# A fused Flamingo block on one core: first alignment part of 12 sequences instead of 16, the second part's dense work as a hand-ordered pipeline with its clamp on GpSimd

## The chip, the core and the metric

The kernel runs on one core of a Trainium2 chip. The core has five engines with in-order queues of their own: TensorE (PE; its weight loads are listed as PEld), VectorE (DVE), ScalarE (ACT), GpSimd (POOL) and SyncE (SP, here only a queue for DMAs). DMAs are issued from SP, ACT and POOL. The metric is device microseconds of one launch; lower is better.

## The reference, cut to what matters

Input are 32 sequences of 128 tokens with 128 features. Four residual steps follow each other, each on the row-normalised state.

```python
x = x + tanh(g_xattn[0]) * mlstm_attention(_layernorm(x), ctx)      # step 1
x = x + tanh(g_ffn[0])   * quantised_ffn(_layernorm(x), W1, b1, W2, b2)   # step 2
x = x + tanh(g_xattn[1]) * align(ctx, _layernorm(x))                # step 3
x = x + tanh(g_ffn[1])   * moe(_layernorm(x), gate_w, w1, b1, w2, b2)     # step 4
```

- Step 2 quantises its input and its hidden values with one scale for the whole tensor: `q = clip(round(h / scale) + zp, -128, 127)`, and multiplies the integers.
- Step 3 is dynamic time warping for every sequence: a 128x128 matrix of distances `sqrt(max(aa + bb - 2 ab, 0))`, the recursion `R[i,j] = d[i,j] + min(R[i-1,j], R[i,j-1], R[i-1,j-1])`, and a backtrack along the cheapest path, which adds context rows to tokens.
- Step 4 is a mixture of 8 experts (128 to 512 to 128 with gelu). Every expert is computed for every token. The gate keeps logits from a k-th value upwards, and that k-th value is taken over all tokens, so gates are known only when step 3 is done for all 32 sequences.

## The kernel before, in words

Sequences are handled in groups of four (`GB`), eight groups (`NG`). Features or hidden units lie on the 128 partitions; `X` holds the state, `YT` the transposed normalised state, `CT` and `CD` the context.

Up to 228 us steps 1 and the first half of step 2 are done for all 32 sequences. Then the sequences are split: the first `NP` groups (4 before, 16 sequences) are the first part, the rest the second.

1. **First dense part** (`dense_steps`, with `dense`, `norm_steps`, `take` and `distances`). For each group of the first part: quantise 128x2048 hidden values (`HT`) on DVE (L905), ACT (L908) and DVE (L909), multiply on PE (L915), add to `X` on DVE (L920), normalise (L153 to L209), transpose, make distances on PE (L930, L932) and their roots on ACT (L938 to L941), and write these to DRAM (`d_dram`, L944).
2. **First warp** (`warp_steps`). Every sequence is worked from both ends, so the recursion has 64 rows (`SH`), and both halves of n sequences lie on 2n partitions. Rows come in `CHUNKS`. Each row is two DVE instructions that depend on each other: a minimum (L1035) and a scan (L1036). The distances of a chunk are loaded by DMA (`dc`, L1019). After a chunk, its rows (`ru`) are spread by four DMAs over 128 partitions (`rblk`, L1045), DVE works out step lengths in a few wide instructions (`dg`, `to`, `lf`, `vv`, `dv`, L1061 to L1074; called a block here) and DMAs bring them back (L1076). `rblk` is a single buffer. After the last row `meet` joins the two halves (PE L978 and L984, copies `gt` and `far` on ACT, L981 and L990, ten small DVE instructions). Then 63 DVE instructions walk back (`hit`, L1084), and `ends` is worked out through PE (L1092 to L1106).
3. **Second dense part** (`quiet`), issued beside the first warp. It leaves DVE alone: ACT does the whole quantisation in four passes of 128x2048 (L1151, L1153, L1155, L1156), PE multiplies (L1160), ACT scales (`t`, L1165), GpSimd adds to `X` (L1167), ACT takes mean and square sums (L1173, L1177), GpSimd the root (L1181 to L1183), ACT normalises (L1187), PE transposes (L1190), and `distances` follows. One group starts when the one before has finished its roots.
4. **Mixture of experts.** `aligned(g)` applies the path to group g and gives its logits. Then PE runs 64 units (expert times group), 8 experts for the first part's groups and 8 for the second's. Second warp, alignments of the other groups and the search for the k-th value are fed in between as a background (`pump`), with a budget in microseconds per step given by `yield`. Results of the first `HELD` units go to DRAM until the gates are known.

What sets the order: every engine executes its queue strictly in the order in which a planner, which orders instructions by estimated times, has put them; `tc.issue_after(...)` ties an instruction behind another. An instruction that waits holds back everything behind it on its queue, also where it is a DMA on ACT's or SP's queue.

Of the kernel before, what the change touches and what calls it, by code (L numbers as in the profile page):

```python
# [18 lines left out]
P = 128  # L19
B = 32  # L20
# [13 lines left out]
SH = S // 2  # L34
CHUNKS = ((0, 16), (16, 16), (32, 16), (48, 8), (56, 8))
NP = 4
BP = NP * GB
HELD = 32


@with_exitstack
def tile_flamingo_gated(
# [747 lines left out]
    parts = [ExitStack(), ExitStack()]  # L790
    HT = [None, None]
    for k in (1, 0):
        HT[k] = new(
            pool(parts[k], f"ffn{k}", side="right"), [P, NC, (B - BP if k else BP) * S], F32, f"HT{k}"
        )
    with ExitStack() as st:
# [18 lines left out]
        with ExitStack() as st2:  # L815
# [26 lines left out]
            for n in range(4):  # L842
                for c in range(NC):
                    ph = new(p_h, [P, 2, 512], F32, "ph")
                    for k in range(2):
                        o = 1024 * n + 512 * k
                        nc.tensor.matmul(  # L847
                            ph[:, k, :], lhsT=w1q[:, c * P : (c + 1) * P], rhs=XQ[:, o : o + 512],
                            start=True, stop=True,
                        )  # L850
                    k, o = (1, 1024 * n - BP * S) if 8 * n >= BP else (0, 1024 * n)
                    hb = HT[k][:, c, o : o + 1024]
# [49 lines left out]
    def dense(n, tie, dp, po_new, got):  # L902
        blk = HT[0][:, :, 512 * n : 512 * n + 512]
        with tc.issue_after(tie):
# [44 lines left out]
    def dense_steps(tie, dp, lp, po_new, psp, tag, take):  # L949
        ties = [tie, tie]  # L950
        behind = iter(())
        for n in range(NP):
            for _ in dense(n, ties[n], dp, po_new, ties):
                for _ in range(3):
                    next(behind, 0)
            if n % 2 == 1:
                for _ in behind:
                    pass
                behind = norm_steps(lp, psp, GB * (n - 1), 2 * GB, take, tag)
        for _ in behind:  # L960
            pass
# [5 lines left out]
    def warp_steps(s0, n_s, wp, w1p, ps_new, queues, ends_queues, eng, DV, ends, lower):  # L967

        H2 = 2 * n_s
        BL = 1 << (P // H2).bit_length() - 1 if n_s > 16 else 4  # L970
        vw = new(w1p, [H2, SH + 1], F32, "vw")
# [3 lines left out]
        def meet(row):  # L975
# [4 lines left out]
            gt = new(w1p, [P, 2, 2, n_s], F32, "gt")  # L980
            nc.scalar.copy(gt, gt_ps.unsqueeze(2).to_broadcast([P, 2, 2, n_s]))  # L981
            both_ps = ps_new([H2, 2, S], "both_ps")
# [6 lines left out]
            eng.memset(far[:, S : S + 1], BIG)  # L989
            nc.scalar.copy(far[:, 0:S], both_ps[:, 1, :])  # L990
            best = new(w1p, [H2, S], F32, "best")
# [20 lines left out]

        for r0, n in CHUNKS:
            if r0 >= SH - 16:
                queues = ends_queues
            dc = new(wp, [H2, 16, S], F32, "dc")[:, 0:n, :]
            for v in (slice(0, 4), slice(4, n)) if r0 == 0 else (slice(0, n),):
# [5 lines left out]

            ru = new(wp, [H2, 17, 2, S + 4], F32, "ru")
            eng.memset(ru[:, :, :, S : S + 4], 0.0)
# [16 lines left out]
            m = n // BL  # L1042
            rb = new(w1p, [P, 16 // BL + 1, 2, S + 4], F32, "rblk")
            for q in range(BL):
# [11 lines left out]

            def block(tag):
                return new(w1p, [P, 16 // BL, S], BF16, tag)[:, 0:m, :]

            dg, to, lf, vv, dv = (block(t) for t in ("dg", "to", "lf", "vv", "dv"))  # L1060
            nc.vector.tensor_tensor(dg, diag, up, ALU.is_le)  # L1061
            nc.vector.tensor_tensor(
                to, jotab.unsqueeze(1).to_broadcast([P, m, S]), dg, ALU.subtract
            )
            nc.vector.tensor_tensor(lf, left, least, ALU.is_lt)
            yield 0.4 * m

# [63 lines left out]
    with ExitStack() as st:  # L1131
        wp = pool(st, "warp", bufs=2, side="right")
        w1p = pool(st, "warp1", side="right")
        dp = pool(st, "distB", side="right")
        lpB = pool(st, "lnB", bufs=2, side="right")
        w_ps = pool(st, "warpps", space=PSUM)
# [5 lines left out]

        room = CD[:, 0:BP].rearrange("p b s -> p (b s)").bitcast(BF16).rearrange(
            "p (k c s) -> p k c s", c=NC, s=GB * S
        )

        def quiet(n):
            grp = slice(GB * n, GB * n + GB)
            blk = HT[1][:, :, 512 * (n - NP) : 512 * (n - NP) + 512]
            with tc.issue_after(held["root"]):  # L1150
                nc.scalar.activation(blk, blk, AF.Identity, bias=magic_c, scale=inv)  # L1151
            hq = room[:, n % 2]
            nc.scalar.activation(hq, blk, AF.Relu, bias=low[:, 1:2])  # L1153

            nc.scalar.activation(hq, hq, AF.Relu, bias=top[:, 0:1], scale=-1.0)  # L1155
            nc.scalar.activation(hq, hq, AF.Identity, bias=top[:, 1:2], scale=-1.0)  # L1156
            po = new(p_o, [P, GB, D], F32, "po")
            for i in range(GB):
                for c in range(NC):
                    nc.tensor.matmul(  # L1160
                        po[:, i, :], lhsT=hq[:, c, i * S : (i + 1) * S], rhs=w2q[:, c, :],
                        start=(c == 0), stop=(c == NC - 1),
                    )
            t = new(lpB, [P, GB, D], F32, "t")
            nc.scalar.activation(t, po, AF.Copy, scale=s2)  # L1165
            xb = X[:, grp, :]
            nc.gpsimd.tensor_add(xb, xb, t)  # L1167

            mean = new(lpB, [P, GB], F32, "mean")
            var = new(lpB, [P, GB], F32, "var")  # L1170
            for i in range(GB):
                y = new(lpB, [P, D], F32, "y", bufs=4)
                nc.scalar.activation(  # L1173
                    y, xb[:, i, :], AF.Identity, scale=-1.0 / D, accum_out=mean[:, i : i + 1]
                )
                y = new(lpB, [P, D], F32, "y", bufs=4)
                nc.scalar.activation(  # L1177
                    y, xb[:, i, :], AF.Square, bias=mean[:, i : i + 1], accum_out=var[:, i : i + 1]
                )
            r = new(lpB, [P, GB], F32, "r")  # L1180
            nc.gpsimd.tensor_scalar(r, var, 1.0 / D, 1e-5, ALU.mult, ALU.add)  # L1181
            nc.gpsimd.tensor_tensor(r, r, minus_half, ALU.pow)
            nc.gpsimd.tensor_tensor(mean, mean, r, ALU.mult)  # L1183
            tp = new(dps, [P, GB, S], F32, "tp")
            for i in range(GB):
                y = new(lpB, [P, D], F32, "y", bufs=4)
                nc.scalar.activation(  # L1187
                    y, xb[:, i, :], AF.Identity, bias=mean[:, i : i + 1], scale=r[:, i : i + 1]
                )
                nc.tensor.transpose(tp[:, i, :], y, ident)  # L1190
            distances(
                n, tp, dp, lambda: new(dps, [P, GB, S], F32, "d2"), (nc.gpsimd, nc.gpsimd)
            )

        for _ in warp_steps(
# [266 lines left out]
```

## Time and profile before

| | us |
|---|---|
| median of 3 runs (876.16 to 877.29) | 876.93 |
| the profiled execution's own time | 880.01 |
| its span in the trace | 878.3 |
| first dense part, from its first DVE instruction to its last root | 228.0 to 267.6 |
| first warp, first scan to `ends` | 272.9 to 380.7 |
| `aligned(0)`, to the first expert matmul | 380.7 to 392.3 |
| mixture of experts, to the end | 392.3 to 878.3 |

The profiled execution is 3.1 us slower than the median of the runs; 1.7 us of its time lie outside the span. Times in the text below are positions in this one execution, and differences worked out from them are applied to the median. In answers by group a line gives the engine, the line of the kernel, the operation, output<-inputs with their shapes, and durations; in a timeline the first number is the start and the second the duration in us, and a bracket tells how long the engine sat idle before and who released it.

### The profile page before, as it was taken

The numbers are of one execution on the slowest core, as the hardware profiler recorded it, in microseconds if no ns is written. First come the engines' busy times: TensorE is split into PE (matmuls) and PEld (weight loads), VectorE is DVE, ScalarE is ACT, GpSimd is POOL, SyncE is SP. The second block draws the span as 40 slices with busy tenths as digits, with TensorE's granted clock in tenths as the row PEclk, the third lists the DMA queues.
The fourth block names the chain that finished last, engine by engine and source line by source line (L and its number), as shares of the span: only waits on it lengthen the run. The fifth ranks groups of instructions, "written<-read, shape, count | busy, mean of one in ns | idle before, by whom it ended". The sixth has DMA issues, their size and how long they took to land.

```text
span 878.3 us, 13244 instructions
## 1 busy us (share of the span) xinstructions
PE 690.1 (79%) x4689; PEld 461.6 (53%) x4695; DVE 571.4 (65%) x2007; ACT 443.7 (51%) x791; POOL 60.9 (7%) x124
## 2 busy tenths in 40 slices
PE   5798998343361323169999999999999999999997
PEld 2244554211341212146677777776677777777775
DVE  7757899979845796969993174656625444445554
ACT  2788677495357673724344444444344433333442
POOL 2000000001201111100000010000010000000000
PEclk9898799655565555559999999999999999999999
DMA  8000000200013322012343120020021121211121
GB/s 318 36 2 12 1 3 1 97 1 0 1 24 66 81 56 49 13 36 68 98 105 120 40 88 37 26 83 37 25 84 40 46 85 37 85 37 37 49 73 49
DMA packets 21613, 47.03 MB, mean 54 GB/s; under 512 B 4626, under 2 KB 8466, under 8 KB 21394
## 3 DMA queue, kind: packets, MB, share of 16 engines
q1 hardware_dynamic: 15592, 29.59, 11.6%
q0 software_dynamic: 4800, 15.83, 5.7%
q10 hardware_dynamic: 1154, 0.76, 0.4%
q8 instruction: 37, 0.61, 0.3%
q14 instruction: 30, 0.25, 0.1%
HBM read 26.59 MB, written 12.85 MB: 45 GB/s over the span
## 4 chain that ended last, share of the span: by engine, by line
PE 54%; DVE 17%; ACT 4%; issue 2%; DMA 1%; POOL 1%; ACTq 0%; SPq 0%; DVEq 0%
PE mph L1390 24%; PE mpo L1403 23%; DVE ru L1036 4%; DVE ru L1035 3%; DVE hst L857 2%; DVE hst L858 2%; PE d L930 1%; PE px L1233 1%; PE small L1253 1%; PE po L915 1%; PE d L932 1%; PE px L1247 1%; DVE junk L1267 1%; DVE bn L153 1%; DMA rblk<-ru 1%
## 5 line engine op out<-in xcount | busy, mean ns | idle before, releaser
L1403 PEld LDWEIGHTS mpo<-mw,hT 128*128 128x128 f32 x2048 | 249.9, 192 | 59.8 <-issue 41.7
L1395 ACT ACTIVATE hT<-mph,mb1s 128x512 f32<-128x512 f32 x256 | 175.7, 687 | 187.8 <-PE mph L1390 173.7
L1403 PE MATMUL mpo<-mw,hT 128*128 128x128 f32 x2048 | 256.1, 276 | 0.1
L1390 PE MATMUL mph<-YT,mw 128*128 128x512 f32 x512 | 245.2, 599 | 0.0
L1390 PEld LDWEIGHTS mph<-YT,mw 128*128 128x128 f32 x512 | 87.2, 193 | 57.3 <-issue 57.2
L1353 DVE TENSOR_TENSOR biased<-mpo,mb2s 128x512 f32<-128x512 f32 x30 | 20.7, 691 | 119.7 <-PE mpo L1403 119.7
L1358 DVE SCALAR_TENSOR_TENSOR X<-biased,GA,X 128x128 f32<-128x128 f32 x248 | 67.7, 345 | 0.1
L1411 ACT COPY ye<-mpo 128x512 f32<-128x512 f32 x32 | 18.7, 585 | 80.9 <-PE mpo L1403 78.3
L1036 DVE TENSOR_TENSOR_SCAN ru<-ru,dc 32x128 f32<-32x128 f32 x128 | 53.7, 420 | 5.5 <-DMA dc<-d_dram 2.2
L1160 PE MATMUL po<-w2q,CD 128*128 128x128 bf16 x64 | 7.5, 312 | 43.1 <-ACT CD L1156 43.1
L1035 DVE TENSOR_TENSOR ru<-ru 32x128 f32<-32x128 f32 x128 | 36.8, 287 | 3.2
L560 ACT ACTIVATE dm<-bi 128x512 f32<-128x512 f32 x48 | 28.9, 605 | 9.2 <-PE bi L555 4.3
L1412 POOL DMA_DIRECT2D y_dram<-ye x32 | 17.4, 543 | 224.3 <-ACT ye L1411 195.2
L602 DVE TENSOR_TENSOR sm<-sc,dm 128x512 f32<-128x512 f32 x32 | 21.7, 683 | 13.7 <-ACT dm L560 9.7
L1160 PEld LDWEIGHTS <-CD 128*128 128x128 bf16 x64 | 6.5, 146 | 44.0 <-ACT CD L1156 44.0
L847 PE MATMUL ph<-XQ,w1q 128*128 128x512 bf16 x31 | 15.2, 604 | 17.1 <-DVE XQ L838 9.6
L1190 PE MATMUL tp<-ident,y 128*128 128x128 f32 x16 | 6.6, 473 | 26.2 <-ACT y L1187 26.2
L1084 DVE SCALAR_TENSOR_TENSOR hit<-jotab,vw,YT 32x128 bf16<-32x128 bf16 x63 | 22.4, 355 | 6.1 <-DMA YT<-dv 3.9
L1084 DVE SCALAR_TENSOR_TENSOR hit<-jotab,vw,CD 32x128 bf16<-32x128 bf16 x63 | 21.4, 340 | 7.1 <-DMA CD<-dv 4.9
L536 PE MATMUL sc<-qm,CD 64*128 64x256 f32 x128 | 22.9, 470 | 0.7 <-ACT YT L377 0.6
L516 ACT ACTIVATE qm<-YT,mcol 128x512 f32<-128x512 f32 x32 | 23.2, 731 | 0.0
L930 PE MATMUL d<-ysq,ones 128*128 128x512 f32 x16 | 15.4, 1060 | 9.3 <-ACT ysq L927 9.3
(363 smaller groups left out, 986.0 us busy)
## 6 DMA issues: line engine op xcount, KB each, us to landing
y_dram<-ye POOLq DMA_DIRECT2D x32, 256.0 KB, 2.3
yl<-y_dram SPq DMA_DIRECT2D x32, 256.0 KB, 2.6
mw<-in_mw POOLq DMA_DIRECT2D x12, 512.0 KB, 4.3
rblk<-ru SPq DMA_DIRECT2D x24, 165.0 KB, 2.7
X<-in_x SPq DMA_DIRECT2D x4, 512.0 KB, 6.1
CD<-in_ctx_d SPq DMA_DIRECT2D x4, 512.0 KB, 7.0
CT<-in_ctx_t SPq DMA_DIRECT2D x4, 512.0 KB, 9.3
mw<-in_mw SPq DMA_DIRECT2D x4, 512.0 KB, 5.1
```

The costliest lines, as they stand in the source:

```text
L516: nc.scalar.activation(held["qm", g][:, h], YT[:, GB * g : GB * g + GB, :], AF.Copy, scale=mcol[:, h : h + 1],)
L536: nc.tensor.matmul(scs[:, k, 4 * v : 4 * v + 4], lhsT=CD[kr, n, :], rhs=qm[kr, :, n % GB, SH:S], start=True, stop=True,)
L560: done = nc.scalar.activation(dm, bi, AF.Exp)
L602: got = nc.vector.tensor_tensor(sm, scs[:, u], dm, ALU.mult)
L930: nc.tensor.matmul(d2, lhsT=ones, rhs=ysq, start=True, stop=False)
L1035: nc.vector.tensor_tensor(u, ru[:, r, 0, 1 : S + 1], ru[:, r, 0, 0:S], ALU.min)
L1036: nc.vector.tensor_tensor_scan(ru[:, r + 1, 0, 1 : S + 1], u, dc[:, r, :], BIG, ALU.min, ALU.add)
L1084: nc.vector.scalar_tensor_tensor(hit, jotab[0:H2], vw[:, r + 1 : r + 2], DV[:, r, :], ALU.is_le, ALU.mult, accum_out=vw[:, r : r + 1],)
L1358: nc.vector.scalar_tensor_tensor(X[:, b, :], v[:, i, :], GA[:, E * b + e : E * b + e + 1], X[:, b, :], ALU.mult, ALU.add,)
L1390: got = nc.tensor.matmul(ph, lhsT=w1e[:, j, c * P : (c + 1) * P], rhs=tok, start=True, stop=True)
L1395: got = nc.scalar.activation(hT[c], ph, AF.Gelu_apprx_tanh, bias=mb1s[:, e, c : c + 1])
L1403: got = nc.tensor.matmul(po[:, i, :], lhsT=hT[c][:, i * S : (i + 1) * S], rhs=w2e[:, j, c, :], start=(c == 0), stop=(c == NC - 1),)
```

## The change

The first part has three groups (12 sequences on 24 partitions), the second five (20 sequences on 40 partitions). Chunks are 12 rows instead of 16, six instead of five. Hidden values lie in four tiles of eight sequences. In the second dense part the last two of ACT's four quantisation passes are replaced by one GpSimd instruction (minimum with 255, then add), two groups are in work at once, and the order on ACT and on PE is tied down instruction by instruction. In the warp the copies `gt` and `far` go from ACT to DVE, and a small ACT copy (`dv`'s first column) goes away, since `vv` now has a leading column of zeros. Blocks of the second warp spread over 80 partitions instead of 128 (`BL` is 2). 34 results are held instead of 32.

```diff
-CHUNKS = ((0, 16), (16, 16), (32, 16), (48, 8), (56, 8))
-NP = 4
+CHUNKS = ((0, 12), (12, 12), (24, 12), (36, 12), (48, 8), (56, 8))
+NP = 3
-HELD = 32
+HELD = 34
...
-            nc.scalar.copy(gt, gt_ps.unsqueeze(2).to_broadcast([P, 2, 2, n_s]))
+            nc.vector.tensor_copy(gt, gt_ps.unsqueeze(2).to_broadcast([P, 2, 2, n_s]))
...
-            nc.scalar.copy(far[:, 0:S], both_ps[:, 1, :])
+            nc.vector.tensor_copy(far[:, 0:S], both_ps[:, 1, :])
...
-            if r0 >= SH - 16:
+            if r0 >= SH - 8:
                 queues = ends_queues
...
-            nc.scalar.copy(dv[:, :, 0:1], vv[:, :, 0:1])
-            nc.vector.tensor_tensor(dv[:, :, 1:S], vv[:, :, 1:S], vv[:, :, 0 : S - 1], ALU.subtract)
+            nc.vector.tensor_tensor(dv, vv[:, :, 1:], vv[:, :, 0:S], ALU.subtract)
...
+        def quantize(n, step):
+            blk, hq = block(n)
+            if step == 0:
+                act(blk, blk, AF.Identity, bias=magic_c, scale=inv)
+                return
+            act(hq, blk, AF.Relu, bias=low[:, 1:2])
+            nc.gpsimd.tensor_scalar(hq, hq, 255.0, low[:, 0:1], ALU.min, ALU.add)
...
+            for n in range(NP, NG):
+                act(t, held["po"], AF.Copy, scale=s2)
+                nc.gpsimd.tensor_add(xb, xb, t)
+                if n + 1 < NG:
+                    quantize(n + 1, 0)
...
+                if n + 1 < NG:
+                    quantize(n + 1, 1)
+                elif d2 is not None:
+                    roots(n - 1, d2)
...
+                if n + 1 < NG:
+                    product(n + 1)
+                if d2 is not None:
+                    roots(n - 1, d2)
...
+                d2 = distance_product(n, ym2, ysq)
+            roots(NG - 1, d2)
```

More of the change, by code (lines that the diff above doesn't have):

```diff
@@ L790, in tile_flamingo_gated @@
     parts = [ExitStack(), ExitStack()]
-    HT = [None, None]
+    HT = [None] * 4
     for k in (1, 0):
-        HT[k] = new(
-            pool(parts[k], f"ffn{k}", side="right"), [P, NC, (B - BP if k else BP) * S], F32, f"HT{k}"
-        )
+        hp = pool(parts[k], f"ffn{k}", side="right")
+        for q in range(3, 0, -1) if k else (0,):
+            HT[q] = new(hp, [P, NC, 8 * S], F32, f"HT{q}")
     with ExitStack() as st:
@@ L850, in tile_flamingo_gated @@
                         )
-                    k, o = (1, 1024 * n - BP * S) if 8 * n >= BP else (0, 1024 * n)
-                    hb = HT[k][:, c, o : o + 1024]
+                    hb = HT[n][:, c, :]
                     nc.scalar.activation(
@@ L902, in dense @@
     def dense(n, tie, dp, po_new, got):
-        blk = HT[0][:, :, 512 * n : 512 * n + 512]
+        blk = HT[n // 2][:, :, 512 * (n % 2) : 512 * (n % 2) + 512]
         with tc.issue_after(tie):
@@ L955, in dense_steps @@
                     next(behind, 0)
-            if n % 2 == 1:
+            if n % 2 == 1 or n == NP - 1:
                 for _ in behind:
                     pass
-                behind = norm_steps(lp, psp, GB * (n - 1), 2 * GB, take, tag)
+                m = n % 2 + 1
+                behind = norm_steps(lp, psp, GB * (n - m + 1), m * GB, take, tag)
         for _ in behind:
@@ L969, in warp_steps @@
         H2 = 2 * n_s
-        BL = 1 << (P // H2).bit_length() - 1 if n_s > 16 else 4
+        BL = 2 if n_s > 16 else 4
+        rows = max(n for _, n in CHUNKS)
+        lft = new(w1p, [BL * H2, rows // BL, S + 1], BF16, "lf")
+        nc.vector.memset(lft[:, :, 0:1], 0.0)
+        tot = new(w1p, [BL * H2, rows // BL, S + 1], BF16, "to")
+        nc.vector.memset(tot[:, :, 0:1], 0.0)
         vw = new(w1p, [H2, SH + 1], F32, "vw")
@@ L1013, in warp_steps @@
         for r0, n in CHUNKS:
-            if r0 >= SH - 16:
+            if r0 >= SH - 8:
                 queues = ends_queues
-            dc = new(wp, [H2, 16, S], F32, "dc")[:, 0:n, :]
+            dc = new(wp, [H2, rows, S], F32, "dc")[:, 0:n, :]
             for v in (slice(0, 4), slice(4, n)) if r0 == 0 else (slice(0, n),):
@@ L1022, in warp_steps @@
                     )
-            ru = new(wp, [H2, 17, 2, S + 4], F32, "ru")
+            ru = new(wp, [H2, rows + 1, 2, S + 4], F32, "ru")
             eng.memset(ru[:, :, :, S : S + 4], 0.0)
@@ L1042, in warp_steps @@
             m = n // BL
-            rb = new(w1p, [P, 16 // BL + 1, 2, S + 4], F32, "rblk")
+            rb = new(w1p, [BL * H2, rows // BL + 1, 2, S + 4], F32, "rblk")
             for q in range(BL):
@@ L1055, in warp_steps, with block @@
             least = rb[:, 1 : m + 1, 1, 0:S]
-            def block(tag):
-                return new(w1p, [P, 16 // BL, S], BF16, tag)[:, 0:m, :]
-            dg, to, lf, vv, dv = (block(t) for t in ("dg", "to", "lf", "vv", "dv"))
+            def block(tag, w):
+                return new(w1p, [BL * H2, rows // BL, w], BF16, tag)[:, 0:m, :]
+            dg, vv, dv = block("dg", S), block("vv", S + 1), block("dv", S)
+            lf, to = lft[:, 0:m], tot[:, 0:m]
             nc.vector.tensor_tensor(dg, diag, up, ALU.is_le)
             nc.vector.tensor_tensor(
-                to, jotab.unsqueeze(1).to_broadcast([P, m, S]), dg, ALU.subtract
+                to[:, :, 1:], jotab[0 : BL * H2].unsqueeze(1).to_broadcast([BL * H2, m, S]), dg, ALU.subtract
             )
-            nc.vector.tensor_tensor(lf, left, least, ALU.is_lt)
-            yield 0.4 * m
+            nc.vector.tensor_tensor(lf[:, :, 1:], left, least, ALU.is_lt)
+            yield (1.6 if BL == 4 else 3.4) * m / 4
             nc.vector.tensor_tensor_scan(
@@ L1134, in tile_flamingo_gated @@
         dp = pool(st, "distB", side="right")
-        lpB = pool(st, "lnB", bufs=2, side="right")
+        lpB = pool(st, "lnB", side="right")
         w_ps = pool(st, "warpps", space=PSUM)
@@ L1141, in tile_flamingo_gated @@
         )
[L1143 to L1157, printed above, removed]
-            for i in range(GB):
[L1159 to L1162, printed above, removed]
-                    )
[L1164 to L1193, printed above, removed]
@@ new lines, in tile_flamingo_gated, with act, block @@
+        room = HT[1][:, :, 0 : GB * S].bitcast(BF16)
+        last = {"act": held["root"], "pe": None}
+        def act(*args, **kw):
+            with tc.issue_after(last["act"]):
+                got = nc.scalar.activation(*args, **kw)
+            last["act"] = getattr(got, "ins", got)
+        def block(n):
+            return (
+                HT[n // 2][:, :, 512 * (n % 2) : 512 * (n % 2) + 512],
+                room[:, :, 512 * (n % 2) : 512 * (n % 2) + 512],
+            )
+        def quantize(n, step):
[5 more added lines that the diff above has]
+            nc.gpsimd.tensor_scalar(hq, hq, 255.0, low[:, 0:1], ALU.min, ALU.add)
+            held["po"] = new(p_o, [P, GB, D], F32, "po")
@@ new lines, in product @@
+        def product(n):
+            hq = block(n)[1]
+            with tc.issue_after(last["pe"]) if last["pe"] is not None else ExitStack():
+                for i in range(GB):
+                    for c in range(NC):
+                        got = nc.tensor.matmul(
+                            held["po"][:, i, :], lhsT=hq[:, c, i * S : (i + 1) * S],
+                            rhs=w2q[:, c, :], start=(c == 0), stop=(c == NC - 1),
+                        )
+            last["pe"] = getattr(got, "ins", got)
@@ new lines, in distance_product @@
+        def distance_product(n, ym2, ysq):
+            d2 = new(dps, [P, GB, S], F32, "d2")
+            with tc.issue_after(last["pe"]):
+                nc.tensor.matmul(d2, lhsT=ones, rhs=ysq, start=True, stop=False)
+                for i in range(GB):
+                    got = nc.tensor.matmul(
+                        d2[:, i, :], lhsT=CD[:, GB * n + i, :], rhs=ym2[:, i, :],
+                        start=False, stop=(i == GB - 1),
+                    )
+            last["pe"] = getattr(got, "ins", got)
+            return d2
@@ new lines, in roots @@
+        def roots(n, d2):
+            dd = new(dp, [P, GB, S], F32, "a")
+            for i in range(GB):
+                b = GB * n + i
+                act(dd[:, i, :], d2[:, i, :], AF.Relu, bias=aa[:, b : b + 1])
+            dist = new(dp, [P, GB, S], F32, "b")
+            act(dist[0:SH], dd[0:SH], AF.Sqrt)
+            act(dist[SH:P], dd[SH:P, :, ::-1], AF.Sqrt)
+            for h in range(2):
+                nc.gpsimd.dma_start(
+                    out=d_dram[h, GB * n : GB * n + GB].rearrange("b r j -> r b j"),
+                    in_=dist[SH * h : SH * h + SH],
+                )
@@ new lines, in second_dense @@
+        def second_dense():
+            d2 = None
+            for step in range(2):
+                quantize(NP, step)
+            product(NP)
+            for n in range(NP, NG):
+                xb = X[:, GB * n : GB * n + GB, :]
+                t = new(lpB, [P, GB, D], F32, "t")
+                act(t, held["po"], AF.Copy, scale=s2)
+                nc.gpsimd.tensor_add(xb, xb, t)
+                if n + 1 < NG:
+                    quantize(n + 1, 0)
+                mean = new(lpB, [P, GB], F32, "mean")
+                var = new(lpB, [P, GB], F32, "var")
+                for i in range(GB):
+                    y = new(lpB, [P, D], F32, "y", bufs=4)
+                    act(y, xb[:, i, :], AF.Identity, scale=-1.0 / D, accum_out=mean[:, i : i + 1])
+                    y = new(lpB, [P, D], F32, "y", bufs=4)
+                    act(
+                        y, xb[:, i, :], AF.Square, bias=mean[:, i : i + 1],
+                        accum_out=var[:, i : i + 1],
+                    )
+                r = new(lpB, [P, GB], F32, "r")
+                nc.gpsimd.tensor_scalar(r, var, 1.0 / D, 1e-5, ALU.mult, ALU.add)
+                nc.gpsimd.tensor_tensor(r, r, minus_half, ALU.pow)
+                nc.gpsimd.tensor_tensor(mean, mean, r, ALU.mult)
+                if n + 1 < NG:
+                    quantize(n + 1, 1)
+                elif d2 is not None:
+                    roots(n - 1, d2)
+                    d2 = None
+                tp = new(dps, [P, GB, S], F32, "tp")
+                for i in range(GB):
+                    y = new(lpB, [P, D], F32, "y", bufs=4)
+                    act(y, xb[:, i, :], AF.Identity, bias=mean[:, i : i + 1], scale=r[:, i : i + 1])
+                    with tc.issue_after(last["pe"]):
+                        got = nc.tensor.transpose(tp[:, i, :], y, ident)
+                last["pe"] = getattr(got, "ins", got)
+                if n + 1 < NG:
+                    product(n + 1)
+                if d2 is not None:
+                    roots(n - 1, d2)
+                ym2 = new(dp, [P, GB, S], F32, "a")
+                act(ym2, tp, AF.Copy, scale=-2.0)
+                ysq = new(dp, [P, GB, S], F32, "b")
+                act(ysq, tp, AF.Square)
+                d2 = distance_product(n, ym2, ysq)
+            roots(NG - 1, d2)
@@ L1199, in tile_flamingo_gated @@
             pass
-        for n in range(NP, NG):
-            quiet(n)
+        second_dense()
     parts[1].close()
```

## The prediction

> **What bounds the kernel now.** I read the page's table of engines, then busy time by stage, then the waits of DVE inside the first warp, then the timeline around GpSimd's instructions.
>
> ```profile
> PE 690.1 (79%) x4689; PEld 461.6 (53%) x4695; DVE 571.4 (65%) x2007; ACT 443.7 (51%) x791; POOL 60.9 (7%) x124
> ```
>
> The stages, each with its length and then busy time of PE, PEld, DVE, ACT and POOL:
>
> ```profile
> 228.00:267.60 39.60, 21.86 (x120) 16.12 (x120) 21.75 (x83) 22.62 (x37) 1.26 (x1) 0.63 0.11 20
> 267.60:380.70 113.10, 31.39 (x131) 20.65 (x131) 85.41 (x305) 68.94 (x139) 15.33 (x22) 0.53 0.22 49
> 380.70:392.30 11.60, 5.02 (x20) 4.24 (x21) 8.55 (x39) 1.22 (x3) 1.35 (x2) 0.50 0.33 68
> 392.30:878.30 486.00, 477.51 (x2744) 345.87 (x2744) 269.73 (x1028) 200.40 (x303) 23.92 (x44) 0.99 0.20 61
> ```
>
> From 392.3 on PE is busy 477.5 of 486.0 us: the experts are bound by PE. Before that, from 267.6 to 380.7, DVE is the busiest (85.4 of 113.1) and carries the first warp. ACT has 68.9 us there, and its second dense part (267.65 to 382.3, four groups of 27.1) runs beside it and ends with it. So the end moves with the moment at which the first `ends` are there, as long as PE gets no new stalls among the experts.
>
> ```profile
> DVE dg L1061 <- DMA rblk<-ru: 4.6, 2, 2.4
> DVE hit L1084 <- DMA YT<-dv: 3.9, 1, 3.9
> DVE ev L1096 <- PE vt L1092: 3.3, 1, 3.3
> DVE best L992 <- ACT far L990: 3.2, 1, 3.2
> ```
>
> These are DVE's waits in the warp (us in total, times, longest). DVE also loses time while it counts as busy:
>
> ```profile
> 332.31 0.28 DVE L1035 TENSOR_TENSOR ru<-ru 32x128 f32<-32x128 f32 x1
> 332.60 1.25 POOL L1167 TENSOR_TENSOR X<-X,t 128x512 f32<-128x512 f32 x1 [9.99 <-ACT t L1165]
> 332.62 1.52 DVE L1036 TENSOR_TENSOR_SCAN ru<-ru,dc 32x128 f32<-32x128 f32 x1
> ...
> 365.26 1.25 POOL L1167 TENSOR_TENSOR X<-X,t 128x512 f32<-128x512 f32 x1 [10.00 <-ACT t L1165]
> ...
> 365.39 1.27 DVE L1084 SCALAR_TENSOR_TENSOR hit<-jotab,vw,YT 32x128 bf16<-32x128 bf16 x1
> ```
>
> A scan of 0.41 takes 1.52 and a `hit` of 0.34 takes 1.27, both just while GpSimd adds to `X`. The minimum at 278.73 (1.38 instead of 0.28) is a third case; the fourth addition, at 305.41, met DVE waiting for `rblk`. So an addition of 1.25 costs the warp 1.11 us at most.
>
> [...] 2.14 ns per element, from 1.256 us at 512 and 2.354 us at 1024 elements (L869).
>
> **The change part by part**, on the profiled time axis.
>
> *1. Earlier start of the warp: -3.7.* Without the fourth group its roots go. Group 3's (the third's) roots end at 264.99, the fourth's at 267.65: -2.66. On DVE, L905, L909 and L920 of the fourth group go (about 1.2 + 0.66 + 0.67 by start distances), partly replaced by waits for PE; following the queue I get the first normalised row at 244.1 instead of 245.61: -1.5. On SP one more distance load (chunk two, first half) stands ahead of the second half's first load: one issue, 0.42 by L1019's median. First scan: 272.94 - 2.66 - 1.5 + 0.42 = 269.2.
>
> *2. Row recursion: 67.0 to 59.4 without GpSimd.* Before it runs from 272.94 to 339.98. 64 rows of 0.763 (48.8) stay, since their cost follows the 128 columns and not the partitions. The two waits for `rblk` go, -4.6: the first block now stands six rows (4.6 us) behind the end of its chunk, and `rblk` lands 2.85 after it (285.9 to 288.75). Blocks of four block rows take 3.1, of two 1.63, so of three 2.37: ahead of the meeting 4 x 2.37 = 9.5 instead of 3 x 3.1 + 1.63 = 10.9, -1.4. One more chunk: a copy 0.31 and memsets 0.2, +0.5. Two stretched instructions leave for part 3, -2.2.
>
> *3. GpSimd: +14.4, of which 2.2 were there.* Additions: 5 x 1.11 = 5.5. The clamp of 128x2048 bf16 is not in this trace. Its nearest row is AFFINE_SELECT, one input: 288 ns at 128 and 666 ns at 512 elements, 0.98 ns per element, so 2.2 us. [...] upper: the addition's two-input rate, 1.256 + 1536 x 0.00214 = 4.55. I take 2.2. By the addition's example DVE loses all but 0.15 of it. The first clamp follows two ACT passes after the last root (263.5 + 4.2) and ends near 269.9, 0.7 into the recursion; the other four lie in it: 0.7 + 4 x 2.05 = 8.9. [...] Less than nothing is excluded: no DVE work is taken away by the clamp.
>
> Meeting: 269.2 + 59.4 + 14.4 = 343.0, instead of 340.0.
>
> *4. From the meeting to the first `hit`: 10.8 to 15.6.* `gt` and `far` on DVE save the ACT queue's delay, about 0.9: `best` starts 2.3 after the last scan. But only the last chunk now uses both queues, and two blocks stand behind the meeting instead of one. By the order of the queues: six small operations (1.65), then chunk five's `dg`, `lf`, `to`, and on to its `dv`, at +6.1. SP then issues its four `dv` DMAs (0.59 each, +8.5), and only behind them the third slice of chunk six's `rblk`, which lands about 2.5 later (+11.0). The block (1.6) gives +12.6, two `dv` issues per queue and landing (1.2 + 1.9) give +15.7; rounded 15.6. Bounds 11.5 (only the second block added) and 17.5.
>
> *5. Walk and `ends`: 29.9 to 26.0.* The stretched `hit` goes, -0.9; PE is free when `vt` comes, so of the 3.3 some 0.4 stay, -2.9.
>
> `ends`: 343.0 + 15.6 + 26.0 = 384.6 instead of 380.7: **+3.9**.
>
> *6. The pipeline itself: nothing on the path.* A group on ACT becomes t 0.67, two passes 4.1, sums 3.3, normalising 1.65, roots 2.4, `ym` and `ysq` 1.1: 13.3 us instead of 27.1. But ACT's queue also holds the last distance load, which waits for row 48 on DVE; ACT gets there near 309 and stands until about 322. Behind it wait only second-part activations and GpSimd's additions. ACT still finishes near 365, and its next customer is the second warp after 392. The cover is the walk; if it were gone, ACT would add its tail of 8 us.
>
> *7. Experts: 0.* Unit count and PE work stay. Fewer units (24 instead of 32, 7.0 us each) cover second warp and alignment. By adding PE's durations in queue order, `vt` of the second warp comes 160 us after the first unit instead of 144. DVE had 10.3 us of waiting there, loses one alignment (8.5) and gains 13.5 for blocks twice as deep. So no stall is due; bound +4. The held results (34 instead of 32) move 2 copies of 0.59 on ACT and 2 x 256 KB, beside PE.
>
> Sum: +3.9 on 880.01, the profile's own time; the median stands 3.1 lower, so 876.93 + 3.9, about **881.0**.
>
> **The rivals.**
>
> *Faster (0.19): the clamp does not block.* [...] For it: no one-input GpSimd instruction of length runs beside two-input DVE work in this trace. Against: three additions block fully. Then -8.9: 872.0 (869.5 to 875).
>
> *Slower and larger (0.15, part of the slower side): the clamp runs at 3.2 us or more*, up to 4.55, so +4 to +11.6 more: 885 to 892. Above 3.3 it also stops fitting beside ACT's 5.2 us between passes and the next product.
>
> *About the same (0.13): small errors meet.* [...]
>
> *Experts starve.* DVE comes late to `vt`, PE stalls us for us. It decides once DVE is over 10 us later than its slot; price up to 4. It is in the range, not in the centre.
>
> *The pipeline does not pipeline*, because the load in ACT's queue stops it. I expect that stop; it costs nothing, since ACT is not the bound.
>
> **How the numbers follow.** Blocking at about 2.2 us: 0.53, time 881.0, own range 878.7 to 884. With 0.15 for the long clamp this makes slower 0.68; same 0.13; faster 0.19. About 0.2%, 1.8 us, is what a measurement of this kernel can tell from no change. The range 869.5 to 889.0 takes in the non-blocking case and a clamp of up to about 4 us.
>
> **What would show it.** Scans and minima of 2 us and more beside each clamp, five of them; first scan near 269; last scan near 343; DVE waiting for `rblk` behind the meeting; first `hit` some 15 us after the last scan; no wait of `ev` for PE; ACT idle for over 10 us at its distance load. I am wrong in the main step if scans beside the clamps stay at 0.41, or if the first unit starts before 390.

## The result, and the profile after

The changed kernel takes **890.1 us** (median of 4 runs, 889.1 to 893.6) against 876.9; the ratio is 1.016, 95% interval 1.013 to 1.019. That is slower, as forecast, but by 13.2 us instead of 3.9, and 1.1 us beyond the top of the range.

The profiled execution took 890.56 us, with a span of 888.8. First the line of busy time by engine, then busy time by stage (length, then PE, PEld, DVE, ACT, POOL), the stages cut as before the change: first dense part, warp up to `ends`, up to the first expert, experts.

```profile
PE 686.7 (77%) x4695; PEld 458.9 (52%) x4695; DVE 604.9 (68%) x2020; ACT 434.8 (49%) x793; POOL 102.5 (12%) x137
```

```profile
225.00:259.40 34.40, 16.89 (x90) 12.28 (x90) 17.52 (x71) 17.41 (x28) 1.27 (x1) 0.68 0.08 16
259.40:390.90 131.50, 36.17 (x161) 23.95 (x161) 108.00 (x317) 64.60 (x155) 57.09 (x35) 0.54 0.19 42
390.90:402.50 11.60, 5.08 (x21) 4.30 (x21) 8.57 (x40) 0.59 (x1) 0.00 (x0) 0.50 0.00 0
402.50:888.80 486.30, 477.62 (x2744) 345.98 (x2743) 285.12 (x1040) 201.51 (x298) 25.03 (x46) 0.99 0.21 65
```

The first dense part is 5.2 us shorter and the experts are as long as before (486.3 against 486.0). The warp is 18.4 longer (131.5 against 113.1), and two engines grew in it together: POOL by 41.8 us busy, DVE by 22.6. DVE has hardly more instructions (317 against 305), so single ones became longer. DVE's longest waits behind the first scan (us in total, times, longest):

```profile
DVE dg L1070 <- DMA rblk<-ru: 5.1, 2, 4.9
...
DVE hit L1092 <- DMA YT<-dv: 3.1, 1, 3.1
...
DVE far L998 <- PE both_ps L992: 1.1, 1, 1.1
```

These three come to 9.3 us, against 15.0 for the four waits shown before, so the added time isn't a wait that DVE's queue shows. The groups inside the row recursion (busy, mean ns) show it:

```profile
L1043 DVE TENSOR_TENSOR ru<-ru 24x128 f32<-24x128 f32 x63 | 37.3, 592 | 2.0
L1044 DVE TENSOR_TENSOR_SCAN ru<-ru,dc 24x128 f32<-24x128 f32 x64 | 30.1, 470 | 5.3 <-DMA dc<-d_dram 3.2
L1172 POOL TENSOR_SCALAR HT<-HT,low 128x2048 bf16<-128x2048 bf16 x5 | 36.1, 7229 | 37.9 <-ACT HT L1157 37.7
```

A row's minimum (L1043) has a mean of 592 ns where 280 is its usual duration, and the clamp (L1172) takes 7.2 us. The timeline, DVE and GpSimd alone, joins the two:

```profile
280.41 0.28 DVE L1043 TENSOR_TENSOR ru<-ru 24x128 f32<-24x128 f32 x1
280.73 0.41 DVE L1044 TENSOR_TENSOR_SCAN ru<-ru,dc 24x128 f32<-24x128 f32 x1
280.76 7.35 POOL L1172 TENSOR_SCALAR HT<-HT,low 128x2048 bf16<-128x2048 bf16 x1 [0.30 <-ACT HT L1157]
281.17 4.49 DVE L1043 TENSOR_TENSOR ru<-ru 24x128 f32<-24x128 f32 x1
285.69 0.41 DVE L1044 TENSOR_TENSOR_SCAN ru<-ru,dc 24x128 f32<-24x128 f32 x1
```

The minimum that starts behind the clamp ends at 285.66, 4.9 us into the clamp, and from there DVE runs at its usual pace although GpSimd works until 288.11. The five clamps stretch one instruction each: a scan by 2.63 and four minima by 4.21, 4.20, 4.22 and 4.23, together **19.5 us**.

All stages below are in us, read from the profiled execution of each kernel and counted from the first DVE instruction of the first dense part. That instruction stood anywhere from 224.4 to 233.7 in these executions, for reasons ahead of all the edits, so stages tell more than the totals of single executions. Each row is one execution; experiment 5 is not in the table, since only its durations are used.

| kernel | first scan | recursion (first to last scan) | last scan to first `hit` | first `hit` to `ends` | behind `ends` |
|---|---|---|---|---|---|
| before | 44.9 | 67.0 | 10.8 | 29.7 | 497.8 |
| after | 40.5 | 82.4 | 17.0 | 25.8 | 498.1 |
| 1 clamp on ACT | 41.1 | 63.1 | 17.1 | 26.7 | 497.4 |
| 2 clamp on DVE | 40.6 | 65.7 | 15.5 | 25.8 | 497.6 |
| 3 before, clamp on GpSimd | 44.9 | 81.3 | 11.1 | 30.4 | 497.6 |
| 4 clamp in four pieces | 41.1 | 74.3 | 31.6 | 25.8 | 497.2 |
| 6 as 1, two chunks on both queues | 40.6 | 64.5 | 10.6 | 27.1 | 501.6 |
| 7 as 1, two `rblk` | 39.3 | 74.4 | 9.5 | 26.7 | 498.0 |
| 8 before, copies by DVE | 45.7 | 66.8 | 9.9 | 31.7 | 497.5 |
| 9 as 2, two chunks on both queues | 40.8 | 67.5 | 10.3 | 25.8 | 497.8 |
| 10 as 1, no set order | 40.9 | 62.9 | 19.7 | 25.8 | 498.5 |

### The profile page after: what moved, and what is told of

Read it like the earlier page. It is cut to its first block, busy times and chain, and to the rows that moved or that the text cites. A ratio compares the mean times of both kernels' runs of the same rounds, so it can differ in the third digit from the quotient of the medians.

```text
span 888.8 us, 13258 instructions
## 1 busy us (share of the span) xinstructions
PE 686.7 (77%) x4695; PEld 458.9 (52%) x4695; DVE 604.9 (68%) x2020; ACT 434.8 (49%) x793; POOL 102.5 (12%) x137
## 3 DMA queue, kind: packets, MB, share of 16 engines
q1 hardware_dynamic: 14692, 29.99, 11.1%
## 4 chain that ended last, share of the span: by engine, by line
PE 51%; DVE 21%; ACT 3%; issue 2%; DMA 1%; POOL 1%; SPq 0%; ACTq 0%; DVEq 0%; POOLq 0%
PE mph L1457 23%; PE mpo L1470 23%; DVE ru L1043 4%; DVE ru L1044 3%; DVE hit L1092 2%; DVE hst L858 2%; DVE hst L859 2%; PE px L1300 1%; POOL HT L1172 1%; PE small L1320 1%; DVE bn L155 1%; DVE junk L1334 1%; PE px L1314 1%; PE d L931 0%; PE po L916 0%
## 5 line engine op out<-in xcount | busy, mean ns | idle before, releaser
L1044 DVE TENSOR_TENSOR_SCAN ru<-ru,dc 24x128 f32<-24x128 f32 (+1 forms) x128 | 56.7, 443 | 6.8 <-DMA dc<-d_dram 3.2
L1043 DVE TENSOR_TENSOR ru<-ru 24x128 f32<-24x128 f32 (+1 forms) x128 | 55.6, 434 | 3.4
L1172 POOL TENSOR_SCALAR HT<-HT,low 128x2048 bf16<-128x2048 bf16 x5 | 36.1, 7229 | 37.9 <-ACT HT L1157 37.7
L1180 PE MATMUL po<-w2q,HT 128*128 128x128 bf16 x80 | 9.4, 311 | 34.9 <-POOL HT L1172 34.9
L1250 PE MATMUL tp<-ident,y 128*128 128x128 f32 x20 | 8.2, 475 | 31.6 <-ACT y L1157 31.6
L604 DVE TENSOR_TENSOR sm<-sc,dm 128x512 f32<-128x512 f32 x32 | 21.8, 686 | 13.3 <-ACT dm L562 9.8
L849 PE MATMUL ph<-XQ,w1q 128*128 128x512 bf16 x32 | 15.4, 603 | 17.0 <-DVE XQ L840 9.2
L1180 PEld LDWEIGHTS <-HT 128*128 128x128 bf16 x80 | 8.1, 145 | 36.4 <-POOL HT L1172 36.4
L1092 DVE SCALAR_TENSOR_TENSOR hit<-jotab,vw,YT 24x128 bf16<-24x128 bf16 x63 | 21.4, 340 | 5.3 <-DMA YT<-dv 3.1
L1316 ACT COPY YT<-px 128x512 f32<-128x512 f32 x8 | 4.7, 587 | 39.0 <-PE px L1314 39.0
L1092 DVE SCALAR_TENSOR_TENSOR hit<-jotab,vw,CD 40x128 bf16<-40x128 bf16 x63 | 21.7, 344 | 2.2
```

Source lines behind the costliest of these rows:

```text
L604: got = nc.vector.tensor_tensor(sm, scs[:, u], dm, ALU.mult)
L1043: nc.vector.tensor_tensor(u, ru[:, r, 0, 1 : S + 1], ru[:, r, 0, 0:S], ALU.min)
L1044: nc.vector.tensor_tensor_scan(ru[:, r + 1, 0, 1 : S + 1], u, dc[:, r, :], BIG, ALU.min, ALU.add)
L1092: nc.vector.scalar_tensor_tensor(hit, jotab[0:H2], vw[:, r + 1 : r + 2], DV[:, r, :], ALU.is_le, ALU.mult, accum_out=vw[:, r : r + 1],)
L1172: nc.gpsimd.tensor_scalar(hq, hq, 255.0, low[:, 0:1], ALU.min, ALU.add)
```

## The experiments

The theory: GpSimd's clamp holds DVE's next instruction, and the 19.5 us held so are the whole loss; without them the change would be a gain. The rivals: the split of 12 and its late transfers, the meeting's copies, or the set order of ACT and PE.

### 1 and 2: the clamp taken off GpSimd

```diff
-            nc.gpsimd.tensor_scalar(hq, hq, 255.0, low[:, 0:1], ALU.min, ALU.add)
+            act(hq, hq, AF.Relu, bias=top[:, 0:1], scale=-1.0)
+            act(hq, hq, AF.Identity, bias=top[:, 1:2], scale=-1.0)
```

> The changed kernel with its five clamps given back to ACT (two passes of 2.00 us each, as in the kernel before); the set order of ACT and PE, the split of 12 and the meeting copies by DVE stay. Theory (the GpSimd clamp holds DVE's two-input instructions): the five row minima of 3.0 to 4.5 us return to 0.28 us, so 19.5 us go, to 870.6 us (868.5 to 873); the time from the first scan to the last falls from 82.4 to about 63. Rival A (the split of 12, the meeting copies or the late dv and rblk transfers cost the time): 889 to 892, since none of them is touched. Rival B (what is taken off GpSimd is paid by ACT: 5 x 4.0 us more on ACT in a chain that DVE waits for): 880 to 888, with DVE waiting for ACT's dc transfer or for PE.

```diff
-            nc.gpsimd.tensor_scalar(hq, hq, 255.0, low[:, 0:1], ALU.min, ALU.add)
+            nc.vector.tensor_scalar(hq, hq, 255.0, low[:, 0:1], ALU.min, ALU.add)
```

> The changed kernel with its five clamps on DVE, one pass of 0.75 us each as in the first dense part, placed in DVE's order between rows of the recursion. Theory: 19.5 us of held rows go and 5 x 0.75 = 3.8 us come, so 874.4 us, plus up to 3 us where DVE stands in front of a clamp whose input ACT has not finished: 873 to 878. Rival A (split, copies or transfers): 893 to 896, the clamps being added to an unchanged rest. Rival B (DVE now waits for ACT's chain in every group, 5 times by 3 us or more): 884 to 892.

Measured: 873.8 us on ACT (ratio to before 0.996, 0.9944 to 0.9976) and 874.75 on DVE (0.9956, 0.9939 to 0.9973), against 877.7 of the kernel before on the same chip. The recursion's groups of the first, on ACT:

```profile
L1044 DVE TENSOR_TENSOR_SCAN ru<-ru,dc 24x128 f32<-24x128 f32 x64 | 28.5, 445 | 5.3 <-DMA dc<-d_dram 3.2
L1043 DVE TENSOR_TENSOR ru<-ru 24x128 f32<-24x128 f32 x63 | 17.6, 279 | 2.0
```

The mean of the minimum is back at 279 ns, and the recursion is 19.3 us shorter (63.1, "about 63" was expected). The second total lies inside the bounds given, the first 0.8 above them. Nothing else of the change was touched, so rival A is out for the bulk of the loss; rival B too, since ACT's 20 us more show up in none of DVE's stages (the 0.9 in the walk is an addition of `X` that now falls there). On DVE the clamp costs what it lasts, 0.73 us: 63.1 and four clamps of 2.9 together make the 65.7 within 0.3.

### 3: the clamp alone, in the kernel before

```diff
-            nc.scalar.activation(hq, hq, AF.Relu, bias=top[:, 0:1], scale=-1.0)
-            nc.scalar.activation(hq, hq, AF.Identity, bias=top[:, 1:2], scale=-1.0)
+            nc.gpsimd.tensor_scalar(hq, hq, 255.0, low[:, 0:1], ALU.min, ALU.add)
```

> The kernel before with one thing of the change: its four clamps, two ACT passes each, become one GpSimd pass each. Theory: each clamp lasts 7.2 us and holds DVE's row minimum for 4.2 us, 4 x 4.2 = 16.8, so 893.7 us (890 to 896); four row minima of about 4.5 us appear. Rival (the clamp costs only together with the set order of ACT and PE or the smaller chunks): 876 to 880, and no row over 1.5 us.

Measured: 893.05 us (ratio 1.0175, 1.0155 to 1.0194), +15.4. The timeline of this kernel, DVE and GpSimd alone, two of its four clamps:

```profile
300.03 7.36 POOL L1155 TENSOR_SCALAR CD<-CD,low 128x2048 bf16<-128x2048 bf16 x1 [3.22 <-ACT dv L1073]
300.08 0.41 DVE L1036 TENSOR_TENSOR_SCAN ru<-ru,dc 32x128 f32<-32x128 f32 x1
300.53 4.41 DVE L1035 TENSOR_TENSOR ru<-ru 32x128 f32<-32x128 f32 x1
...
362.38 7.16 POOL L1155 TENSOR_SCALAR CD<-CD,low 128x2048 bf16<-128x2048 bf16 x1 [3.27 <-ACT CD L1153]
363.07 4.02 DVE L1084 SCALAR_TENSOR_TENSOR hit<-jotab,vw,YT 32x128 bf16<-32x128 bf16 x1 [2.73 <-DMA YT<-dv]
```

The four held instructions lose 3.5, 4.1, 4.2 and 3.7, together 15.5, against a difference of 15.4. That the two agree so closely is in part chance: inside the recursion the waits for `rblk` grew by 2.8 us (7.4 against 4.6), and in the walk `ev`'s wait for PE shrank by 2.9 (0.4 against 3.3). The held instructions are of three kinds, two scans, a minimum and a `hit`: not the row minimum alone is sensitive. The clamp thus holds DVE in the same way without the rest of the change.

### 4: the clamp in four pieces

```diff
-            nc.gpsimd.tensor_scalar(hq, hq, 255.0, low[:, 0:1], ALU.min, ALU.add)
+            for c in range(NC):
+                nc.gpsimd.tensor_scalar(
+                    hq[:, c], hq[:, c], 255.0, low[:, 0:1], ALU.min, ALU.add
+                )
```

> The changed kernel with each clamp cut into four GpSimd instructions of 512 elements, nothing else. Asks what the hold hangs on. If the hold is a share of each instruction (4.8 of 7.2 us, two thirds): 20 pieces of about 1.85 us, each holding DVE for up to 1.2 us, 5 x 4 x 1.0 = 20 us held, 888 to 891. If the last 2.4 us of any clamp are free whatever its length: pieces of 1.85 us hold nothing, 870 to 875. If each piece holds DVE for its whole length, one row slipping in between: 5 x (7.4 - 1) = 32 us held, 900 to 904.

Measured: 896.6 us (ratio 1.0213, 1.0197 to 1.0229), between the cases, and for a reason that none of them named. A piece takes 2.0 us (one took 4.1), all twenty 42.6 against 36.1 for the five whole clamps. A row instruction that is held beside a piece loses 0.3 to 0.5 us and is free about 0.6 into the piece: 1.2, 1.6, 1.3 and 0.3 us for the four clamps inside the recursion. Three pieces of the fourth met a DVE that waited for `rblk`, and the fifth clamp lies behind the last scan, so the fair comparison is that of the first three: 4.1 us instead of 11.0. So the hold is neither a fixed share nor gone. The same trace shows a one-input instruction held, the copy of a row at a chunk's start:

```profile
316.17 1.88 POOL L1225 TENSOR_TENSOR X<-X,t 128x512 f32<-128x512 f32 x1 [3.54 <-ACT t L1157]
...
316.91 1.28 DVE L1040 COPY ru<-ru 24x258 f32<-24x258 f32 x1
```

It usually takes 0.28 us, and ends here 0.15 behind the addition; a second such copy took 0.69 beside a piece. So two inputs are not needed for the hold. The piece of 4.1 us began together with a block of DVE instructions (L1070 to L1082) that ran at their usual durations, so GpSimd can be the one that loses; nothing more was tested on that.

The recursion shrinks by 8.1 to 74.3, although it now contains a wait of 6.7 us for one late `rblk`. But the stretch to the first `hit` grows by 14.6. Its timeline, PE and DVE:

```profile
350.20 0.29 PE L1183 MATMUL po<-w2q,HT 128*128 128x128 bf16 x1 [1.69 <-POOL HT L1173]
...
352.18 1.57 PE L1183 MATMUL po<-w2q,HT 128*128 128x128 bf16 x13 [1.69 <-POOL HT L1173]
...
353.67 0.30 PE L986 MATMUL gt_ps<-ident,ru 24*128 24x24 f32 x1
...
354.01 0.21 DVE L989 COPY gt<-gt_ps 128x48 f32<-128x48 f32 x1 [12.83 <-PE gt_ps L986]
```

PE takes its instructions in order, and the transpose of the meeting (L986) stands behind the product of the last group, which waits for the last clamp's pieces; DVE waits 12.8 us for it, and 5.1 more for `both_ps` behind a distance product. In the changed kernel the last clamp ends at 346.1 and the last scan at 347.9, so the same order just misses the meeting; here the chain ran later and DVE earlier, and PE's order costs about as much as the holds had.

### 5: what sets the 7.2 us

```diff
+            if n == NP:
+                nc.gpsimd.tensor_scalar(hq, hq, 255.0, 0.0, ALU.min, ALU.add)
+            elif n == NP + 1:
+                nc.gpsimd.tensor_scalar(hq, hq, 255.0, None, ALU.min)
+            elif n == NP + 2:
+                nc.gpsimd.tensor_scalar(hq, hq, low[:, 0:1], None, ALU.add)
+            elif n == NP + 3:
+                nc.gpsimd.tensor_scalar(blk, blk, 255.0, low[:, 0:1], ALU.min, ALU.add)
+            else:
+                nc.gpsimd.tensor_tensor(hq, hq, hq, ALU.add)
```

> The changed kernel with five different GpSimd instructions in place of its five clamps, all over 128 x 2048 elements, to see what sets the 7.2 us; the clamp's values are not computed. In order: min and add with two constants; min alone; add of the column alone; min and add in f32 in place (the other four are bf16); an addition of two tensors in bf16. If the second operation is what costs: 7.2, about 3.6, 3.6, 7.2 us. If the per-partition column does: the first two under 4 us, the third 7.2. If bf16 does: the fourth under 5 us, which the addition of X in f32 (512 elements in 1.25 us, so 5.0 us for 2048) would suggest. If it is a price by element whatever the form: all 7.0 to 7.4 us. The two-tensor addition: 5.0 us by the addition of X. The hold of DVE is read beside each: 4.8 us after the start if it is a fixed share of 7.2 us.

The GpSimd groups of the only execution, mean ns behind the comma:

```profile
L1179 POOL TENSOR_SCALAR HT<-HT,low 128x2048 f32<-128x2048 f32 x1 | 7.2, 7249 | 0.1
L1173 POOL TENSOR_SCALAR HT<-HT 128x2048 bf16<-128x2048 bf16 x1 | 7.1, 7107 | 38.0 <-ACT HT L1157 38.0
L1175 POOL TENSOR_SCALAR HT<-HT 128x2048 bf16<-128x2048 bf16 x1 | 5.6, 5577 | 0.3 <-ACT HT L1157 0.3
L1177 POOL TENSOR_SCALAR HT<-HT,low 128x2048 bf16<-128x2048 bf16 x1 | 5.5, 5455 | 0.3 <-ACT HT L1157 0.3
...
L1181 POOL TENSOR_TENSOR HT<-HT 128x2048 bf16<-128x2048 bf16 x1 | 3.7, 3713 | 0.0
```

None of the four expectations holds whole. Neither the number format (7.25 in f32, 7.11 in bf16) nor the column (5.46 with it, 5.58 with a constant) matters here. A second operation adds 1.5 to 1.8 us to a first that takes 5.5. And one input is slower here than two: the addition over as many elements, with the same tile as both inputs, takes 3.71. One rival would be that the clamp is so long because DVE holds it. Experiment 4 speaks against it: the last four pieces ran from 344.2 to 352.1, while DVE waited for `gt_ps`, and took 1.98 to 1.99 us each, as those beside a busy DVE did. The holds: the minimum beside the single operation (L1175) was free after 3.7 us, that beside the addition after 3.6, that beside the f32 form after 4.5. So the addition blocks nearly to its end, the others do not. Why the hold ends where it does is open.

### 6, 7 and 9: the late transfers behind the meeting

The wait of `dg` for `rblk`, 4.9 us after the change and 3.9 with the clamp on ACT, remained. SP's own queue in the changed kernel:

```profile
354.55 2.99 SPq L1084 DMA_DIRECT2D YT<-dv  x4
357.59 0.71 SPq L1053 DMA_DIRECT2D rblk<-ru  x1
```

The fourth issue of chunk five's `dv` ends at 357.54, the slice of `rblk` follows, and `dg` starts at 359.84. The sixth and the ninth edit are one line, on the kernels of the first and the second experiment:

```diff
-            if r0 >= SH - 8:
+            if r0 >= SH - 16:
```

> The first experiment's kernel (clamp on ACT) with the condition of the last chunks' queues as in the kernel before (SH - 16): the transfers of the last two chunks, not of the last alone, go half by SP and half by ACT. Theory (the wait of 3.9 us for rblk after the meeting comes from SP's order, four dv issues ahead of a slice of rblk): last scan to first hit falls from 17.1 to 13 to 14.5 us, so 870.5 us (869.5 to 872) against 873.8. Rival (ACT stands in front of its own transfers until DVE has made the rows, and its delayed groups or late issues cost as much): 873 to 876, with new waits of ACT for DVE's rows.

Measured: 870.45 us (ratio 0.9904, 0.9873 to 0.9935). The total is as expected, its parts are not: last scan to first `hit` falls further, to 10.6 from 17.1, the recursion takes 1.4 more, since chunk five's block now lies in it, and the stretch behind `ends` grew to 501.6. PE there:

```profile
373.34 0.77 PE L1301 MATMUL px<-CT,pt 128*128 128x128 f32 x2 [1.15 <-DVE pt L1300]
373.90 1.92 PE L1190 MATMUL d<-b,ones 128*128 128x512 f32 x2
375.61 1.91 PE L1192 MATMUL d<-a,CD 128*128 128x128 f32 x8
377.31 1.49 PE L1301 MATMUL px<-CT,pt 128*128 128x128 f32 x6
```

With `ends` 5 us earlier the alignment (`px`) meets the second part's last distance product, and its six other products stand 3.4 us behind it.

```diff
-            rb = new(w1p, [BL * H2, rows // BL + 1, 2, S + 4], F32, "rblk")
+            rb = new(wp, [BL * H2, rows // BL + 1, 2, S + 4], F32, "rblk")
```

> The first experiment's kernel with two buffers for rblk instead of one; the queues stay. If the late rblk comes from the single buffer (the transfer of the last chunk cannot start before DVE has read the chunk ahead), the wait of 3.9 us goes and the time is 870 to 871.5. If it comes from SP's order (the dv issues stand ahead of it either way): 873 to 874.5, no difference beyond 0.2%.

Measured: 875.65 us (ratio 0.9967, 0.9947 to 0.9987; the first experiment had 0.996), so two buffers bring nothing. But this is not the clean test that it was meant to be: the planner ordered DVE's blocks anew, the wait behind the meeting went (9.5), and the recursion grew to 74.4, with three waits for `rblk` of up to 2.4 us (7.0 together), one of 1.4 for the transfers of `dv`, and chunk five's block inside it. The single buffer by itself stays open.

> The second experiment's kernel (clamp on DVE) with the queues of the last two chunks as in the sixth. In the sixth, PE's last distance product, late by the long ACT groups, stood ahead of the first products behind the ends, and what follows the ends took 501.6 us instead of 497.5. With the clamp on DVE, ACT's groups end some 20 us earlier, so that goes: last scan to first hit 10.5 to 12 us, the stretch behind the ends 497.5, to 869 us (867.5 to 870.5). Rival (the queues' gain is taken back by ACT standing before its own transfers): 872 to 875.

Measured: 871.85 us (ratio 0.9923, 0.9894 to 0.9952), above its bounds; the profiled execution of it took 868.3. DVE's waits:

```profile
DVE hit L1092 <- DMA YT<-dv: 3.0, 1, 3.0
DVE HT L1172 <- ACT HT L1157: 2.2, 2, 1.3
...
DVE X L1302 <- PE px L1300: 1.1, 1, 1.1
...
DVE dg L1070 <- DMA rblk<-ru: 0.3, 1, 0.3
```

`rblk` is in time, and `px` is waited for 1.1 us instead of 4.5, so behind `ends` 497.8 are back. DVE now stands twice before a clamp whose input ACT has not finished. The sixth and the ninth beat both kernels, the one before by 1.0% and 0.8%; their intervals overlap, and which of them is the faster is open.

### 8 and 10: the copies and the set order

```diff
-            nc.scalar.copy(gt, gt_ps.unsqueeze(2).to_broadcast([P, 2, 2, n_s]))
+            nc.vector.tensor_copy(gt, gt_ps.unsqueeze(2).to_broadcast([P, 2, 2, n_s]))
...
-            nc.scalar.copy(far[:, 0:S], both_ps[:, 1, :])
+            nc.vector.tensor_copy(far[:, 0:S], both_ps[:, 1, :])
```

> The kernel before with one thing of the change: the meeting's two copies, gt and far, by DVE instead of ACT. Theory: DVE's wait of 3.2 us for ACT's far and what ACT's order adds ahead of gt shrink to the wait for PE, while DVE pays two copies of 0.2 to 0.3 us: last scan to first hit 10.8 down to about 8.5, 874.5 to 876 us. Rival (the last rblk and dv transfers run beside the meeting and end as late as before): 876.5 to 878, with the difference turning up in the wait for rblk or YT.

Measured: 879.75 us (ratio 1.0016, 0.9996 to 1.0036): no difference shown. Last scan to first `hit` gives back 0.9 of the 3.2 that DVE waited for `far`, and 2.0 more turn up behind the walk, where DVE waits 2.7 us for PE's `ends_ps` instead of 1.0.

```diff
-            with tc.issue_after(last["act"]):
+            with tc.issue_after(held["root"]):
...
-                    with tc.issue_after(last["pe"]):
+                    with ExitStack():
```

(the second line likewise for the two kinds of product)

> The first experiment's kernel (clamp on ACT) without the set order of the second part's instructions on ACT and PE: only the first of each group stays behind the last root, and the planner mixes the groups. The prediction held the pipeline to be hidden beside DVE's recursion: then 872.5 to 875, as the first experiment, with DVE's stretches unchanged to 1 us. Rival (the set order keeps PE free for the meeting and ACT for its transfers): DVE waits 3 us or more for PE at the meeting, or for rblk, and the time is 877 or more.

Measured: 874.6 us (ratio 0.9967, 0.9948 to 0.9986), as the first experiment. The recursion is 62.9 against 63.1. Up to the first `hit` it takes 2.6 us more, with a wait of 4.9 for `rblk` instead of 3.9, the walk takes 0.9 less, and the stretch behind `ends` 1.1 more. The expectation that DVE's stretches stay unchanged to 1 us did not hold, but no gain in time from the set order is shown.

## Why the prediction was right or wrong, by its steps

| step | predicted | measured |
|---|---|---|
| 1 first scan, against before | -3.7 | -4.4 |
| 2 recursion without GpSimd | 59.4 | 59.0 |
| 3 clamps / additions of `X` | 8.9 / 5.5 | 19.5 / 4.9 |
| 4 last scan to first `hit`, without the addition | 15.6 | 16.0 |
| 5 first `hit` to the end of `ends` | 26.0 | 26.0 |
| 6 and 7 pipeline, experts | 0 | 0.3 |

The measured 59.0 is 82.4 less the 19.5 and the 3.9 of additions that fell into the recursion; the fifth addition, 1.0, fell behind the last scan. That a row costs the same on fewer partitions is borne out: where nothing held it, the minimum took 0.28 and the scan 0.41 on 24 partitions as on 32 before. By the columns such an instruction does grow: over 128 x 512 elements an f32 TENSOR_TENSOR took 0.68. Against the forecast the steps differ by -0.7, -0.4, +10.6, -0.6, +0.4, 0 and +0.3, together +9.6. Up to rounding this is the 13.6 us by which the sums of the stages differ, less the forecast 3.9; the medians differ by 13.2.

**The step that failed is part 3, the size of the clamp.** That DVE is held was right: five stretched instructions, one beside each clamp (3.04 to 4.51 us), and otherwise only those beside the additions (1.17 to 1.41). The price was taken from rows that select by position and do no arithmetic on the data, giving 0.98 ns per element and 2.2 us:

```profile
L351 POOL TENSOR_SCALAR_AFFINE_SELECT mneg<-mneg 128x512 bf16<-128x512 bf16 x2 | 1.3, 666 | 0.0
masks.py:199 POOL TENSOR_SCALAR_AFFINE_SELECT ident<-ident 128x128 f32<-128x128 f32 x1 | 0.3, 288 | 0.0
```

The clamp's own kind, TENSOR_SCALAR, stood in the trace before at 1 and 4 elements only, too few for a price per element. The upper bound was wrong too: it took two inputs for the dearest case, 4.55 by the addition's 2.14 ns per element (1.256 us at 512 elements, 2.354 at 1024), while the clamp took 7.2. It has one input but two operations, and experiment 5 shows a single one at 5.5 us already above the addition's 3.7. That one input costs less than two was the author's estimate from the select rows; 5.5 us for 2048 elements is 2.7 ns each, against their 0.98.

A second error in the same step worked the other way. DVE was to lose all of the clamp but 0.15, by the example of the additions; it lost 4.2 of 7.2. That the block lasts the whole instruction holds nearly for the additions (0.9 to 1.1 of 1.3 us) but not for the clamp, in whose last 2.4 us DVE runs freely. With the clamp blocking to its end, 5.4 and four times about 7.0 us would have been lost, 33 instead of 19.5: about 904, as an estimate.

So the rival that came nearest is "slower and larger", at a chance of 0.15. That its 885 to 892 held the 890.1 is luck as to the price: its clamp was to last at most 4.55 us and block whole, and a clamp of 7.2 that blocks for 4.2 comes to about the same. The range stopped at a clamp of about 4.

Two smaller slips bear on no step. 876.93 + 3.9 is 880.8, not 881.0. And the four groups on ACT before the change were not all of 27.1 us: the third took 32.7, with ACT standing at the meeting's transfers and copies.

**Part 4** came within 0.4 us, and its cause, `dv` issues on SP ahead of a slice of `rblk`, agrees with SP's queue and with experiments 6 and 9. Only the queue's condition was undone there, so it is the split over two queues that is shown to matter; the single buffer is not ruled out as a part of it.

**Part 6** was right in its sum and off in its sizes. ACT stood at its distance load for 5.6 us instead of over 10, because its groups came later: they took 17 to 21 us instead of 13.3. ACT waited 15.5 us in two waits for the product behind a clamp, and 14.9 in three waits of up to 6.2 until it could refill `b`, the buffer of the distances. The store of `b` is issued by GpSimd, and in the two longest of these three waits it stood behind the clamp of the next group (issued at 305.3 and 346.0, as clamps ended at 305.4 and 346.1). No stage of DVE shows a cost of this; its recursion, the cover, was itself longer.

## What to carry to other kernels

Before work goes to GpSimd beside a DVE that is the bound, price it by a row of the same instruction kind on GpSimd; where the trace has none, the upper bound must stay open, and measuring the operation alone costs less than the error. What such an instruction costs a DVE that is the bound is its hold on DVE's next instruction, here 4.2 of 7.2 us, not its own length; what is queued behind it on GpSimd, stores too, waits for its end, as the stores of `b` did here behind the clamps that ended at 305.4 and 346.1. A chain that is hidden beside another engine can still stand ahead of the bound's own work in PE's order, where DVE waited 12.8 us in experiment 4: ask what is next in that queue if the chain is a few us late, or the bound a few us early.

## What the runs showed of the hardware that was not expected

- GpSimd over 128 x 2048 elements: 7.2 us for two operations on one input, in bf16 and f32 alike, 5.5 for one operation (bf16), and 3.7 for a bf16 addition with one tile as both inputs.
- The hold does not go by the instruction's length: DVE was released 4.4 to 4.6 us after the start of 7.2 (two operations), 3.6 to 3.7 of 5.5 (one), 3.6 of 3.7 (the addition), and about 0.6 of 2.0 for a two-operation piece of 512 elements (each from the end of the held instruction less its usual duration). Pieces took 18% longer than the whole clamps in all and, over the first three clamps, held DVE's rows for less than half as long (4.1 against 11.0).
- A copy on DVE with one input was held by an addition on GpSimd as the two-input instructions were: 1.28 us instead of 0.28 (experiment 4).
